# Four weight loads and eight context loads in another order on one DMA queue (a four-layer gated cross-attention kernel)

## The chip, the core and the metric

One Trainium2 chip, one of its cores. The time is device microseconds for one execution of the whole program. The kernel before took 2381.88 us, the median of three runs (2378.09 to 2385.84). One more execution was profiled and took 2372.64 us; every duration below is from that one.

## The reference

Sixteen sequences of 56 tokens with 256 channels pass four layers. Each layer adds a gated cross-attention to a context of 1500 positions with 64 channels for each sequence, and then a gated feed-forward part. Layers 0, 2 and 3 have a mixture of experts as feed-forward part, layer 1 an fp8-quantised matrix. What matters here is the seam inside layer 0 and what follows it:

```python
x = x + tanh(g_xattn[0]) * L0_xattn(layernorm(x), ctx_512, ...)
x = x + tanh(g_ffn[0])   * L0_ffn(layernorm(x), ...)
x = x + tanh(g_xattn[1]) * L1_xattn(layernorm(x), ctx_512, ...)

def L0_ffn(x):            # 16 experts, 4 for each token, and a shared expert for all tokens
    shared  = silu(x @ W1s.T) * (x @ W3s.T) @ W2s.T
    probs   = softmax(x @ Wg.T)
    combine = the four largest of probs, in place, 0 elsewhere
    h       = silu(x @ W1[e].T) * (x @ W3[e].T)          # every expert e
    return shared + sum over e of (h * combine[e]) @ W2[e].T
```

Layer 0's attention is causal and looks at the first 56 context positions only. Layers 1 to 3 look at all 1500, with a rotary embedding applied to the context first.

## The kernel before

The tokens lie as eight tiles of 112 (two sequences of 56 each), in SBUF all through the program (`x`). `kv` holds the whole context in SBUF, eight pairs of sequences, each 125 partitions by 1536 numbers (750 KB); each pair has one load.

**Layer 0's attention** (`attention_mha`) is a hand-written pipeline. Its loop `for i in range(NT + 1)` has nine turns; turn i makes scores of tile i and finishes tile i - 1, and moves the router of earlier tiles forward one phase at a time. Nearly every instruction is pinned with `in_order`, so an engine runs them in the order of the program text. Layer 0's attention needs only the small `k0` part of the context.

**The load queue.** Nearly all loads are issued by SyncE (SP), on one queue, in program order, while SP runs ahead of the compute: it waits only for room in the queue, for the completion of the load eight places before (there are eight completion semaphores for this queue, used in turn), and for buffers to come free. The order in layer 0 is: the tokens and small weights; sixteen clears of the DRAM table `rows` (`clear_rows`, L1177); in turn 2 the cosine and sine tables (`load_tables`, L889 and L890) and pairs 0 and 1; in turn 3 pairs 2 and 3; in turn 4 pairs 4 and 5 and then twelve head weights of layer 1 (`load_absorbed`, L233); in turn 5 pairs 6 and 7 (`load`, L893). Behind these `moe` issues the four loads of the shared expert, and then the experts' weights.

**Layer 0's experts** (`moe`). At its head the object `Shared` is made: it opens a pool "sw" on the right side of SBUF and issues four loads, gate/up weights `swgu` (L1413) and down weights `swd` (L1414) for two halves of the shared expert. The shared expert's work is cut into parts (`sh.parts`): `multiply` (L1429), `activate` (L1440, L1441) and `down` (L1446, L1448). The parts of the first four tiles are laid between the last phases of the router: `tail` holds the routers of tiles 4, 5 and 6, 7, which still have their transposes (L1062), logits (L1070), ranks, place counts (L1106, L1108) and scatters (L1121, on GpSimd) to do. The order at the seam is written out by hand:

```python
next(last); next(before); next(last); next(before)
now[0][0]()                      # shared expert, multiply: 8 matmuls on swgu, L1429
next(before)
for _ in range(4): next(last)    # last pair's transposes L1062, logits L1070, softmax
now[1][0]()
```

When the router has finished, `table` makes a list of expert tiles (up to 128 tokens of one expert). SP reads it (L1200) and loads for each tile the expert's weights `wgu` and `wd` (L1212, L1213), three tiles ahead, and the tile's rows `xrow` (L1219), which must wait for the scatters. TensorE turns the rows (L1226) and multiplies (L1238). Beside the tile loop DVE applies the rotary embedding to the context: `Roping.parts` (L901, L906, L909) takes the pairs in order 0 to 7. The head weights of layer 1 are used after the loop.

The pool "rope" is opened before everything of layer 0 and closed when layer 0 is done; it holds the two tables and a scratch tile.

Of the kernel before, what the change touches and what calls it, by code (L numbers as in the profile page):

```python
# [36 lines left out]
F32 = mybir.dt.float32  # L37
# [8 lines left out]
B, S, D = 16, 56, 256  # L46
# [19 lines left out]
def bcast(ap, axis, n):  # L66

    ap = ap.unsqueeze(axis)
    shape = list(ap.shape)
    shape[axis] = n  # L70
    return ap.to_broadcast(shape)
# [3 lines left out]
def flamingo_kernel(ctx: ExitStack, tc: tile.TileContext, d: dict, out: bass.AP):  # L75
    nc = tc.nc
# [9 lines left out]
    in_order = tc.keep_in_program_order  # L86
# [71 lines left out]
    class Normed:  # L158


        def __init__(self, pool):
            self.pool, self.kept = pool, {}
# [75 lines left out]
    def load_absorbed(l, g):  # L238
        loaded[l, g] = [
            load_heads(n, d[f"L{l}_{n}"], g)  # L240
            for n in ("wqr", "wkr", "wkc", "wq", "wkv", "wo")
        ]
# [136 lines left out]
                project_turned(*before)  # L379


    def attention_mha(router, roping):
        with ExitStack() as st:
            ap1 = st.enter_context(tc.tile_pool(name="a0c", bufs=1))
            ap = st.enter_context(tc.tile_pool(name="a0", bufs=2))
# [53 lines left out]
            for half in range(2):  # L439
# [4 lines left out]
                i = bcast(ps[0:DC, 0 : 4 * TP].rearrange("p (n s) -> p n s", s=S), 2, 2)  # L444
# [4 lines left out]
            def keys(t):  # L449
                ps = ps_k.tile([128, 512], F32, name="k_ps")[:, 0 : 4 * TP].rearrange("p (q n) -> p q n", q=4)  # L450
                for q in range(4):
                    in_order(nc.tensor.matmul(ps[:, q, :], wk[:, q, :], k0d[:, 2 * t : 2 * t + 2, 0, :], start=True, stop=True))
                made["k", t] = ps

            def keep_keys(t):
                ps = made.pop(("k", t))
                for h in range(4):
                    i = ps[32 * h : 32 * h + 32].rearrange("p q (b s) -> p q b s", b=2)
                    in_order(nc.scalar.copy(kbs[t % 2][32 * h : 32 * h + 32, :, :, h, :], i))

            def make_values(t):
                ps = ps_k.tile([TP, 512], F32, name="vb_ps")
                for b in range(2):
                    in_order(nc.tensor.matmul(
                        ps[:, b * D : (b + 1) * D], k0d[:, 2 * t + b].rearrange("p a s -> p (a s)"), wv, start=True, stop=True
                    ))
                made["v", t] = ps

            def keep_values(t):
                pv = made.pop(("v", t)).rearrange("p (b g a c) -> p b g a c", b=2, g=H // 2, a=2)  # L470
                for a in range(2):
                    in_order(nc.scalar.activation(vbs[t % 2][:, :, :, 16 * a : 16 * a + 16], pv[:, :, :, a, :], AF.Copy, scale=small[0:TP, C_M + a : C_M + a + 1]))
# [13 lines left out]
            def turn_normed(half):  # L486
                for k in range(2):
                    ps = (turns, misc)[k]()
                    for i in range(4):
                        in_order(nc.tensor.transpose(ps[:, i * TP : (i + 1) * TP], xn[:, i, k * 128 : (k + 1) * 128], ident[0:TP, 0:TP]))  # L490
                    copy = nc.vector.tensor_copy if k == 0 else nc.scalar.copy
                    in_order(copy(xnT[:, k, 4 * half : 4 * half + 4, :].rearrange("p t c -> p (t c)"), ps[:, 0 : 4 * TP]))

            def queries(half):
                for q in range(4):
                    ps = (turns, misc)[q % 2]()[:, 0 : 4 * TP]
                    for k in range(2):
                        in_order(nc.tensor.matmul(
                            ps,
                            wq[:, k, q * 128 : (q + 1) * 128],  # L500
                            xnT[:, k, 4 * half : 4 * half + 4, :].rearrange("p t c -> p (t c)"),
                            start=k == 0,
                            stop=k == 1,
                        ))

                    in_order(nc.scalar.mul(qT[:, q, half * 4 * TP : (half + 1) * 4 * TP], ps, 0.25))
# [84 lines left out]
            def route(i, *phases):  # L591

                for k in phases:
                    if (i - k) % 2 == 0 and 0 <= (i - k) // 2 < len(batches):
                        next(batches[(i - k) // 2])
# [3 lines left out]
            def at(i):  # L599
                return pairs[i] if 0 <= i < NT else None  # L600
# [10 lines left out]
            for i in range(NT + 1):  # L611
                new, cur = at(i), at(i - 1)
                if cur:
                    cur.turned()
                route(i, 2, 3, 5)
                if cur:
                    cur.keep_turned()
                if i + 1 < NT:
                    keep_keys(i + 1)
                if new:  # L620
                    keep_values(i)
                route(i, 4)
                if new:
                    new.scores()
                route(i, 3, 4)
                if new:
                    new.shift()
                    new.exps()
                if cur:
                    cur.values()  # L630
                route(i, 5)
                if cur:
                    cur.normalize()
                if i + 2 < NT:
                    keys(i + 2)
                if cur:
                    cur.turn_context()
                if i + 1 < NT:
                    make_values(i + 1)
                route(i, 5, 3, 4, 4)  # L640
                if cur:
                    cur.project()
                    cur.add()
                route(i, 3)
                if i == 0:
                    turn_normed(1)
                    queries(1)
                for _ in range(5):
                    next(clear, None)
                if i == 2:  # L650
                    roping.load_tables(nc.sync)
                if 2 <= i < 6:
                    roping.load(2 * i - 4, nc.sync)
                    roping.load(2 * i - 3, nc.sync)
                if i == 4:
                    load_absorbed(1, 0)
                    load_absorbed(1, 1)
# [224 lines left out]
    class Roping:  # L882
# [9 lines left out]
        def load(self, t, queue):  # L892
            in_order(queue.dma_start(kv[:, t], d["ctx"][t]))  # L893
# [283 lines left out]
            in_order(nc.sync.dma_start(rows[e * CT : (e + 1) * CT].rearrange("c p x -> p c x"), bcast(zero, 1, CT)))  # L1177
            yield

    def moe(r, nxt=None, tail=None, rest=None):  # L1180

        l = r.l
        n_e, ft, nf, top, n_t, n_sure = MOE[l]
# [2 lines left out]
        with ExitStack() as st:  # L1186

            right = st.enter_context(ExitStack())
            side = {"side": "right"} if l == 0 else {}
# [5 lines left out]
            pw, pp = pool("w", 4, **side), pool("", 3, **side)  # L1195
            ps_h = pool("h", 2 if l == 2 else 4, space=PSUM)
            ps_o = pool("o", 2, space=PSUM)
# [74 lines left out]
            if l == 0:  # L1272


                sh = Shared(pool, ps_h, ps_o, side)
                now = [part for e in range(2) for part in sh.parts(e, 0)]
                between = [part for e in range(2) for part in sh.parts(e, 1)]
                before, last = tail
                next(last)
                next(before)  # L1280
                next(last)
                next(before)
                now[0][0]()
                next(before)
                for _ in range(4):
                    next(last)
                now[1][0]()
                for _ in range(3):
                    next(last)
                next(last)  # L1290
                next(last)
                r.table()
            else:
                r.table()
# [42 lines left out]
            if l == 0:  # L1337
# [8 lines left out]
                rest = rest()  # L1346
# [55 lines left out]
    class Shared:  # L1402


        def __init__(self, pool, ps_h, ps_o, side):
            self.ps_h, self.ps_o = ps_h, ps_o
            self.pp = pool("s", 2, **side)
            pw = pool("sw", 1, **side)
            self.w = []
            for e in range(2):  # L1410
                wgu = pw.tile([128, 2, 2, 176], F32, name=f"swgu{e}")
                wd = pw.tile([88, 2, D], F32, name=f"swd{e}")
                in_order(nc.sync.dma_start(wgu, d["L0_wgu"][16 + e]))  # L1413
                in_order(nc.sync.dma_start(wd, d["L0_wd"][16 + e]))  # L1414
                self.w.append((wgu, wd))

        def parts(self, e, half):

# [138 lines left out]
    @contextmanager  # L1557
    def routed(l):
        with tc.tile_pool(name=f"r{l}c", bufs=1) as keep, ExitStack() as temporary:
            yield Router(l, keep, temporary)  # L1560

    with tc.tile_pool(name="rope", bufs=1) as rope, routed(0) as r:
        roping = Roping(rope)
        tail = attention_mha(r, roping)
        nxt = Next(1)
        moe(r, nxt, tail, roping.parts)
    with ExitStack() as keep:
        f1w = keep.enter_context(tc.tile_pool(name="f1w", bufs=1, reuse_waits="tile"))
        matrix = f1w.tile([128, 2, D], F32, name="w8"), f1w.tile([128, 4], F32, name="sc")
# [3 lines left out]
        nxt = Next(2)  # L1573
# [7 lines left out]
    with routed(2) as r:  # L1581
        attention_mla(2, nxt, r)
        nxt.whole.close()
        nxt = Next(3)
# [152 lines left out]
```

## Time and profile before

| | |
|---|---|
| median of three runs | 2381.88 us |
| the profiled execution | 2372.64 us |
| its span | 2370.8 us |
| mean granted TensorE clock | 0.971 |
| PE busy | 2226.7 us (94%) |
| DVE busy | 1556.8 us (66%) |
| ACT busy | 1232.3 us (52%) |
| POOL busy | 342.8 us (14%) |
| SP queue (q1), share of 16 DMA engines | 21.6% |
| bytes moved by DMA | 172.97 MB, mean 73 GB/s |

PE is TensorE, PEld its weight load (which overlaps PE), DVE VectorE, ACT ScalarE, POOL GpSimd, SPq the issuing of DMAs by SyncE. L12 is line 12 of the kernel. A row of a timeline gives the start in us, the duration in us, the engine, the line, the operation, what it writes and reads, how many instructions are merged, and in brackets how long the engine had been idle before and what ended that. A row of waits gives the waiting line, what it waited for, the sum in us, how often, and the longest. "PEclk" is the clock granted to TensorE as a share of full speed. The last figure of a DMA issue row is not shown for SP, so landing times are read from who waits for them.

### The profile page before, as it was taken

How to read it: one execution, taken by the hardware profiler on the slowest of the kernel's cores; microseconds unless marked ns; L12 is line 12 of the kernel's file. 1: busy time of each engine (PE TensorE's matmuls, PEld its weight loads, DVE VectorE, ACT ScalarE, POOL GpSimd, SP SyncE). 2: the span in 40 equal slices, each digit the busy share in tenths (PEclk: the TensorE clock that was granted, in tenths of full speed). 3: DMA queues.
4: the chain of work that ended last, by engine and by line, in shares of the span. 5: the costliest groups of instructions: out<-in, count | busy, mean ns of one | idle time of the engine just before them, and what ended most of it. 6: DMA issues, size and time to landing. Idle time of an engine off the chain costs nothing. (4 is left out here: it accounts for less than half of the span.)

```text
span 2370.8 us, 47911 instructions
## 1 busy us (share of the span) xinstructions
PE 2226.7 (94%) x17853; PEld 1603.2 (68%) x17858; DVE 1556.8 (66%) x3594; ACT 1232.3 (52%) x2703; POOL 342.8 (14%) x676
## 2 busy tenths in 40 slices
PE   8859998999999999999999999979899999999797
PEld 5626655777777775447777777745577777777454
DVE  5727545777777777667777777724577777777222
ACT  4403336666666663356666666513566666665131
POOL 1223600000000003420000000001001111111223
PEclk9769999999999999989999999999999999999799
DMA  9546761000000002200000000055101000000597
GB/s 244 184 138 193 207 166 64 9 22 21 22 21 22 21 23 69 66 17 22 23 24 13 21 22 23 11 202 159 34 21 30 29 20 26 25 28 16 158 289 209
DMA packets 114891, 172.97 MB, mean 73 GB/s; under 512 B 19258, under 2 KB 77635, under 8 KB 113628
## 3 DMA queue, kind: packets, MB, share of 16 engines
q1 hardware_dynamic: 105510, 151.35, 21.6%
q0 software_dynamic: 7600, 17.14, 2.2%
q8 instruction: 144, 2.36, 0.4%
q10 hardware_dynamic: 1542, 1.34, 0.2%
q14 instruction: 95, 0.78, 0.1%
HBM read 131.24 MB, written 40.48 MB: 72 GB/s over the span
## 5 line engine op out<-in xcount | busy, mean ns | idle before, releaser
L745 ACT ACTIVATE p<-s_ps,nm 128x500 f32<-128x500 f32 x504 | 335.7, 675 | 361.9 <-DVE nm L736 361.9
L722 PE MATMUL s_ps<-kvT,qT 64*128 64x500 f32 x2016 | 484.2, 607 | 11.4 <-ACT p L754 4.8
L796 PEld LDWEIGHTS m_ps<-pT,kv 125*64 125x64 f32 x8064 | 436.7, 137 | 65.8 <-issue 57.4
L734 DVE TENSOR_REDUCE part<-s_ps 128x1 f32<-128x500 f32 x504 | 340.3, 678 | 213.4 <-PE s_ps L722 213.0
L796 PE MATMUL m_ps<-pT,kv 125*64 125x128 f32 x8064 | 477.3, 275 | 1.8 <-ACT pT L789 1.2
L722 PEld LDWEIGHTS s_ps<-kvT,qT 64*128 64x128 f32 x2016 | 186.8, 189 | 196.1 <-issue 121.6
L784 PE MATMUL m_ps<-ident,p 128*125 128x128 f32 x2016 | 297.4, 282 | 0.2
L739 DVE TENSOR_REDUCE nm<-s_ps 128x1 f32<-128x1500 f32 x168 | 287.2, 1710 | 1.2 <-PE s_ps L722 1.2
L784 PEld LDWEIGHTS m_ps<-ident,p 128*125 128x125 f32 x2016 | 247.5, 187 | 35.5 <-issue 26.0
L754 ACT ACTIVATE p<-s_ps,nm 128x1500 f32<-128x1500 f32 x168 | 254.9, 1517 | 0.5 <-DVE nm L739 0.4
L784 PE MATMUL s_ps<-ident,p 128*125 128x128 f32 x2016 | 248.8, 273 | 0.3 <-ACT p L745 0.3
L784 PEld LDWEIGHTS s_ps<-ident,p 128*125 128x125 f32 x2016 | 233.7, 188 | 1.2 <-ACT p L745 0.5
L789 ACT COPY pT<-s_ps 125x512 f32<-125x512 f32 x336 | 181.0, 596 | 98.3 <-PE s_ps L784 82.3
L765 POOL TENSOR_TENSOR den<-den 128x1 f32<-128x1 f32 x168 | 32.7, 194 | 1210.2 <-ACT p L745 1209.9
L789 ACT COPY pT<-m_ps 125x512 f32<-125x512 f32 x336 | 185.2, 617 | 0.0
L807 DVE TENSOR_TENSOR ctxT<-m_ps,rep 64x128 f32<-64x128 f32 (+1 forms) x384 | 104.2, 271 | 88.1 <-PE m_ps L796 81.1
L1238 PE MATMUL gu_ps<-wgu,xT 128*128 128x448 f32 (+2 forms) x344 | 141.2, 537 | 20.1 <-DMA wgu<-in_L_wgu 13.7
L1243 DVE TENSOR_TENSOR act<-gu_ps,act 128x224 f32<-128x224 f32 (+2 forms) x78 | 31.2, 400 | 152.4 <-ACT act L1242 152.3
L787 DVE COPY pT<-m_ps 125x512 f32<-125x512 f32 x168 | 116.2, 692 | 10.1 <-PE s_ps L784 0.9
L314 ACT COPY qT<-q_ps 64x224 f32<-64x224 f32 x128 | 71.8, 561 | 97.1 <-PE q_ps L358 60.3
L1263 POOL DMA_INDIRECT results<-y,to x78 | 90.6, 1162 | 203.5 <-ACT y L1262 193.8
L787 DVE COPY pT<-s_ps 125x512 f32<-125x512 f32 x168 | 114.3, 681 | 0.0
(294 smaller groups left out, 2514.7 us busy)
## 6 DMA issues: line engine op xcount, KB each, us to landing
wgu<-in_L_wgu SPq DMA_DIRECT2D x36, 448.0 KB
rows<-zero SPq DMA_DIRECT2D x16, 899.5 KB
kvT<-turned_kv SPq DMA_DIRECT2D x16, 750.0 KB
wgu<-in_L_wgu SPq DMA_DIRECT2D x34, 352.0 KB
rep<-through SPq DMA_DIRECT2D x336, 32.0 KB
xrow<-rows SPq DMA_DIRECT2D x78, 128.5 KB
wgu<-in_L_wgu SPq DMA_DIRECT2D x8, 1024.0 KB
wd<-in_L_wd SPq DMA_DIRECT2D x36, 224.0 KB
```

The lines of the kernel that those rows point to most:

```text
L722: in_order(nc.tensor.matmul(o[:, 0 : 4 * KP], qT[64 * b : 64 * b + 64, t, j * QT : (j + 1) * QT], kvTs[t][64 * b : 64 * b + 64, z * 4 * KP ...
L734: in_order(nc.vector.tensor_reduce(self.part[:, z : z + 1], sp0[z][:, 0 : 4 * KP], AX.X, ALU.max))
L739: in_order(nc.vector.tensor_reduce(self.nm[1], sp1[:, :, 0 : 4 * KP], AX.XY, ALU.max, negate=True))
L745: in_order(nc.scalar.activation(self.p[0][:, 4 * z * KP : 4 * (z + 1) * KP], sp0[z][:, 0 : 4 * KP], AF.Exp, bias=self.nm[0], accum_out=sel ...
L754: in_order(nc.scalar.activation(self.p[1].rearrange("p (z c) -> p z c", z=3), sp1[:, :, 0 : 4 * KP], AF.Exp, bias=self.nm[1], accum_out=se ...
L784: in_order(nc.tensor.transpose(ps[:, c, :], self.p[b][:, k : k + KP], ident))
L787: in_order(nc.vector.tensor_copy(o, ps))
L789: in_order(nc.scalar.copy(o, ps))
L796: in_order(nc.tensor.matmul(self.pv[64 * b : 64 * b + 64, :], kv[:, self.t, c, b, :], self.pT[:, c, b, :], start=c == 0, stop=c == KC - 1))
L807: in_order(nc.vector.tensor_tensor(ctxs[self.t][64 * a : 64 * a + 64, b, lo - 448 * a : hi - 448 * a], self.pv[64 * b : 64 * b + 64, cols] ...
L1238: in_order(nc.tensor.matmul(ps[:, s, 0:n], xT[:, k, :], wgu[:, k, s * n : (s + 1) * n], start=k == 0, stop=k == 1))
L1263: i = nc.gpsimd.indirect_dma_start(flat, bass.IndirectOffsetOnAxis(ap=to[:, 0:1], axis=0), y, None, bounds_check=B * S * top - 1, oob_is_e ...
```

## The change

`Shared` is split in two. Its weight tiles are now made in the pool "rope" when the program begins (`__init__`), its four loads are issued by a method `load`, and what is left (`begin`) opens the pool for the intermediate tiles where the object was made before. The attention of layer 0 calls `sh.load()` in turn 2, ahead of the two tables. The context's pairs have new turns: pair 0 in turn 3, pair 1 in turn 4 (ahead of the head weights), pairs 2 and 3 in turns 5 and 6, pairs 4 and 6 in turn 7, pairs 5 and 7 in turn 8. The right-side pool "sw" is gone, and "rope" is 9,728 bytes per partition larger (two tiles of 2,816 bytes and two of 2,048). The instructions of PE, DVE, ACT and POOL and their order stay as they are; only SP's order differs.

```diff
-    def attention_mha(router, roping):
+    def attention_mha(router, roping, sh):
...
                 if i == 2:
+                    sh.load()
                     roping.load_tables(nc.sync)
-                if 2 <= i < 6:
-                    roping.load(2 * i - 4, nc.sync)
-                    roping.load(2 * i - 3, nc.sync)
+                if i > 2:
+                    roping.load(i - 3, nc.sync)
+                    if i > 6:
+                        roping.load(i - 1, nc.sync)
                 if i == 4:
                     load_absorbed(1, 0)
                     load_absorbed(1, 1)
...
-                sh = Shared(pool, ps_h, ps_o, side)
+                sh.begin(pool, ps_h, ps_o, side)
...
     class Shared:
-        def __init__(self, pool, ps_h, ps_o, side):
+        def __init__(self, keep):
+            self.w = [
+                (keep.tile([128, 2, 2, 176], F32, name=f"swgu{e}"), keep.tile([88, 2, D], F32, name=f"swd{e}")) for e in range(2)
+            ]
+
+        def load(self):
+            for e, (wgu, wd) in enumerate(self.w):
+                in_order(nc.sync.dma_start(wgu, d["L0_wgu"][16 + e]))
+                in_order(nc.sync.dma_start(wd, d["L0_wd"][16 + e]))
+
+        def begin(self, pool, ps_h, ps_o, side):
             self.ps_h, self.ps_o = ps_h, ps_o
             self.pp = pool("s", 2, **side)
-            pw = pool("sw", 1, **side)
-            self.w = []
-            for e in range(2):
-                wgu = pw.tile([128, 2, 2, 176], F32, name=f"swgu{e}")
-                wd = pw.tile([88, 2, D], F32, name=f"swd{e}")
-                in_order(nc.sync.dma_start(wgu, d["L0_wgu"][16 + e]))
-                in_order(nc.sync.dma_start(wd, d["L0_wd"][16 + e]))
-                self.w.append((wgu, wd))
...
-        roping = Roping(rope)
-        tail = attention_mha(r, roping)
+        roping, sh = Roping(rope), Shared(rope)
+        tail = attention_mha(r, roping, sh)
...
-        moe(r, nxt, tail, roping.parts)
+        moe(r, nxt, tail, roping.parts, sh)
```

More of the change, by code (lines that the diff above doesn't have):

```diff
@@ L1178, in clear_rows, with moe @@
             yield
-    def moe(r, nxt=None, tail=None, rest=None):
+    def moe(r, nxt=None, tail=None, rest=None, sh=None):
         l = r.l
```

## The prediction

> **What bounds the kernel now.** I read the page's slices first, then the waits of layer 0, then that stretch in windows and as a timeline, and last the load queue (SP) by itself.
>
> ```profile
> PE   8859998999999999999999999979899999999797
> DMA  9546761000000002200000000055101000000597
> ```
>
> One digit is 59.3 us (2370.8 / 40). PE is near full nearly everywhere, so TensorE bounds the kernel over most of the span; the lowest digit is slice 2, 118.5 to 177.8 us, the joint between layer 0's attention and its experts. The waits of the first 182 us name its hole:
>
> ```profile
> PEld sgu_ps L1429 <- DMA swgu<-in_L_wgu: 24.3, 1, 24.3
> PE sgu_ps L1429 <- DMA swgu<-in_L_wgu: 24.2, 1, 24.2
> ```
>
> One wait of 24.2 us, for the shared expert's gate/up weights. The windows (us, then busy time of PE, PEld, DVE, ACT, POOL, then the TensorE clock, DMA share, GB/s) show how empty it is:
>
> ```profile
> 110.00:115.00 5.00, 2.71 (x6) 1.36 (x6) 4.76 (x12) 1.90 (x3) 2.20 (x4) 0.50 0.60 203
> 120.00:125.00 5.00, 0.00 (x0) 0.00 (x0) 0.41 (x2) 0.00 (x0) 3.76 (x5) 0.50 1.00 254
> 135.00:140.00 5.00, 0.00 (x0) 0.00 (x0) 0.00 (x0) 0.00 (x0) 0.00 (x0) 0.50 0.31 129
> ```
>
> Only POOL does anything, and that ends by 129 us. Nothing runs beside this wait that could keep the time up. The timeline gives its edges:
>
> ```profile
> 116.30 0.53 PE L1108 MATMUL m_ps<-total,ones 112*112 112x16 f32 x2
> ...
> 119.67 0.73 DVE L1054 TENSOR_SCALAR xr<-x,mv,y 112x256 f32<-112x256 f32 x2
> ...
> 128.38 0.33 POOL L1064 COPY xr<-small 112x4 f32<-112x4 f32 x2
> 141.04 5.80 PE L1429 MATMUL sgu_ps<-xnT,swgu 128*88 128x448 f32 x8 [24.21 <-DMA swgu<-in_L_wgu]
> ...
> 156.79 0.93 POOL L1121 DMA_INDIRECT rows<-xr,sloti  x1 [28.08 <-issue]
> ...
> 179.09 0.38 PE L1226 MATMUL m_ps<-ident,xrow 128*128 128x128 f32 x2
> ```
>
> PE stops at 116.83 and resumes at 141.04. Behind the stopped matmul stand, on PE in order, the transposes of the last routed tokens (L1062), so the router's end, the table, and every expert tile are late with it. Why the weights are late is in the queue's own timeline:
>
> ```profile
> 66.01 17.70 SPq L893 DMA_DIRECT2D kv<-in_ctx  x6
> 83.76 14.27 SPq L233 DMA_DIRECT2D wqr<-in_L_wqr  x1
> ...
> 119.42 0.33 SPq L233 DMA_DIRECT2D wkr<-in_L_wkr  x1
> ...
> 121.75 0.81 SPq L893 DMA_DIRECT2D kv<-in_ctx  x2
> 122.68 0.35 SPq L1413 DMA_DIRECT2D swgu<-in_L_wgu  x1
> ...
> 170.51 2.97 SPq L1219 DMA_DIRECT2D xrow<-rows  x4
> ```
>
> They are issued at 122.68, last of all, behind two tables, eight context pairs of 750 KB and twelve head weights. wqr's 14.27 us of issuing is the queue being full. In the instruction listing each load also waits for the completion of the one eight places before it; SP's waits show 9.8 us of that (two waits on pairs), the last let go at 119.42.
>
> **The change, part by part.**
>
> *The four shared loads to the front.* They now stand directly behind the 16 row clears, at the place where the cosine table was issued at 62.62 us. The clears' rate lasts until about 71 us (244 GB/s, then 140 from 72). 2 x (352 + 176) KB = 1.08 MB at 244 GB/s take 4.4 us: landed by about 76, some 40 us before PE asks at 116.8. The whole 24.2 us wait goes. Nothing before 116 us waits for a table, a pair or a head weight, so what they are pushed back by costs nothing there.
>
> *What is late next.* (1) The shared matmul's other input, the first half of xnT, was made before the copy at 104.3 us that served the third pair of tiles, and the last a0 PSUM reader ends at 106.7; so it starts at 116.85. Its 8 matmuls take 5.80 us: until 122.65. (2) The transposes behind it need xr, ready at 120.40 and not moved: 2.2 us of margin. (3) POOL's scatters of the last pair (first at 156.79, so 132.6 after) need POOL, free at 128.71: margin 3.9 us. (4) The tile table comes from DVE, 159.5 before, 135.3 after; from there chain and queue order are as before. So everything from 141.04 on moves by 24.2 us, if the loads keep up.
>
> *The context behind them.* Queue order becomes: shared, tables, pairs 0 and 1, twelve head weights, pairs 2, 3, 4, 6, 5, 7. SP runs ahead of the compute, so "a turn each" changes order only, no start time. All the bytes are the same, so the backlog ends about when it did: traffic ran until about 142.5. What changes is who is last: a context pair, whose first reader (roping on DVE, 182.16 before, 158 after) takes the pairs one by one from number 0. But the expert weights (issued at 160.57 before, 136.4 after) and rows (170.51; 146.3 after) stand behind the pairs.
>
> [...] The row: at 135 to 140, when only pairs remain, the DMA share is 0.31 at 129 GB/s, that is five of 16 engines. [...] From landing times (pairs 4 and 5 let waits go at 112.91 and 119.42) it is 6.5 us with scatters beside it. I take 6.5. After: 71 + 4.4 (shared) + 6 (tables) + 2 x 6.5 + 4 (head weights) = 98, + 6 x 6.5 = 137; by equal bytes 142. SP is done issuing well before: the queue held about three pairs when wqr got in, so near 137 - 3 x 6.5 = 118, against 135.3.
>
> First expert weights then land 2 to 4 us after the last pair, about 141 to 146, needed at 179.94 - 24.2 = 155.7. First rows: before, issued 170.51, read by DVE at 172.84, needed by PE at 178.9; so after, needed by 154.7. Three tiles' weights (1.62 MB, a sixteenth per engine at 129/5 = 26 GB/s) add 3.9 us and the row load 2.3: the last pair must be down by 148.5. Margin 6 to 11 us. In the tile loop itself PE waits for wgu 6.8 us in six waits (180 to 320), but its loads are let go by the four weight buffers, so that loop moves as a whole. Cost taken: 0; bounds 0 and, if both estimates are 10 us low, 4.
>
> *Clock.* Row: 0.50 at 110 to 115, with PE half busy, so PE was already cold before the stop. [...] I take the row. Other end: the warm stretches of 148 to 156 and 170 to 180 come cold, about +10 us.
>
> *The pool.* 9,728 bytes per partition move from the right side into the rope pool, which ends with layer 0; left pools shift. Instruction order on PE, DVE, ACT and POOL is unchanged; a few releases differ (one later kvT load also waits for POOL; ACT's first kvT copies lose a wait). SP's waits at that load were 1.0 us in all, for a load fetched ahead: 0, bounds -1 and +1.
>
> Sum: -24.2. The profiled execution took 2372.64 us (span 2370.8): it would take 2348.4. The median of the runs shown is 2381.88, 9.2 higher; the hole does not depend on that, so 2381.88 - 24.2 = **2357.7 us**.
>
> **Rivals.** *Context tail takes part:* pairs need about 10 us each, the last lands near 160, rows come 12 us late: 2370. For it: five engines, last scatters beside them. Against: 6.5 us measured under scatters. *Another releaser:* the wait is put to the load that came last, but POOL ended at 128.7; if the matmul or what follows needs it, 141.0 - 128.7 = 12.3 gained: 2369.6. Against: the matmul reads only xnT and the weights. *Cold clock:* 24.2 - 10 = 14: 2368. *Slower:* the same tail, whole: one place, the expert loads behind pairs on five engines. It eats everything when the last pair lands 24.2 us past 148.5, at 172.7, (172.7 - 98) / 6 = 12.4 us a pair; at 13.5 us, 7 more: 2388. That is twice the row.
>
> **How the numbers follow.** Forecast 0.76, its own range 2347 to 2367 (runs shown spread 8 us); context tail 0.08; other releaser 0.06; cold clock 0.04; tail that cancels the gain 0.03; slower 0.03. A measurement tells about 0.3%, 7 us, from no change. Faster 0.94, same 0.03, slower 0.03. The three partial cases lie at 2368 to 2370, so the range is 2345 to 2372.
>
> **What would show it.** Right: no wait of L1429 on swgu, its first matmul at about 117, the last routing transposes near 122.5, first expert matmul near 156, shared loads down by 80; traffic near 130 GB/s until about 140. Wrong: PE waiting at L1226 or L1238 for xrow or wgu, SP still issuing pairs past 136, or a new hole between 117 and 156.

## The result, and the profile after

The change is faster, but by about half of what was forecast: 2369.18 us (median of 4 runs, 2367.27 to 2373.49) against 2383.86 us for the kernel before on the same chip (4 runs, 2378.09 to 2387.71). The ratio on record is 0.9949, 95% interval 0.9929 to 0.997, which is 12.2 us (7 to 17). It is an estimate over all the runs and not the quotient of the two medians, which lie 14.7 us apart. The forecast was 24.2. The profiled execution took 2373.49 us (span 2371.7, clock 0.972).

The page's slices of the changed kernel (59.3 us each, counted from 0) already say that the hole is not filled as it should be. Slice 2 of PE was 5 before:

```profile
PE   8878998999999999999999999979899999999697
DMA  9647561000000002200000000064001010000596
```

It rose to 7 only, and slice 3 fell from 9 to 8. The waits of the first 182 us of the changed kernel (engine, line, what it waited for, sum in us, times, longest) name no wait for `swgu` any more. They name others in its place:

```profile
PE m_ps L575 <- DVE sum_p L1079: 6.6, 3, 5.0
...
DVE den L569 <- remote: 5.5, 1, 5.5
...
DVE mx L537 <- remote: 5.1, 2, 3.6
...
PE m_ps L1142 <- DVE weight L1172: 3.8, 1, 3.8
...
DVE sloti L1119 <- DMA rows<-xr,sloti: 2.0, 1, 2.0
```

"remote" is a semaphore whose updater the profile does not show; `den` and `mx` are VectorE instructions that wait for TensorE's values (L561) and scores (L523). TensorE's own timeline at these two places:

```profile
89.85 0.72 PE L561 MATMUL m_ps<-vb,pT 112*64 112x34 f32 x19
91.03 0.19 PE L561 MATMUL m_ps<-vb,pT 112*64 112x34 f32 x1 [0.45 <-issue]
91.73 0.29 PE L561 MATMUL m_ps<-vb,pT 112*64 112x34 f32 x3 [0.51 <-issue]
93.17 0.26 PE L561 MATMUL m_ps<-vb,pT 112*64 112x34 f32 x2 [1.14 <-issue]
94.57 0.66 PE L561 MATMUL m_ps<-vb,pT 112*64 112x34 f32 x7 [1.14 <-issue]
...
115.23 1.93 PE L561 MATMUL m_ps<-vb,pT 112*64 112x34 f32 x32
122.14 0.66 PE L575 MATMUL m_ps<-ident,ctx 128*128 128x128 f32 x2 [4.98 <-DVE sum_p L1079]
...
128.65 6.10 PE L1434 MATMUL sgu_ps<-xnT,swgu 128*88 128x448 f32 x8
```

In other turns the 32 values matmuls take 1.08 to 1.93 us in one group. Here they come in five, with 3.2 us of gaps that nothing in the profile explains ("issue"). Behind the last group of L561 TensorE stands 4.98 us, where it stands 0.91 in the traces of both kernels on chip 8 below. It waits there for VectorE, whose `den` waits 5.5 us until 121.27, although the matmuls that it needs seem done at 117.16; why is not in the profile. I call these the two **holds**. The trace of the kernel before that the prediction was made from has neither. The sixth turn (from its L549 to the next) lasted 10.2 us there and 15.8 here, and from the last turn's L549 to the first shared matmul being ready it was 12.8 there and 16.6 here. That is 9.4 us; another 2.8 were there before the sixth turn (TensorE's clock was 0.50 from 60 to 65 us here and 1.00 before). Together with 0.4 us regained between, the shared expert began at 128.65 us and not at 116.85: it waited for nothing, and still came 11.8 us late. So the change saved 141.04 - 128.65 = 12.4 us there, between these two profiled executions. The weights were not what it was late for.

### The profile page after: what moved, and what is told of

It reads as the page before. It is cut to its first block, busy times and chain, and to the rows that moved or that the text cites. A ratio compares the mean times of both kernels' runs of the same rounds, so it can differ in the third digit from the quotient of the medians.

```text
span 2371.7 us, 47925 instructions
## 1 busy us (share of the span) xinstructions
PE 2234.8 (94%) x17858; PEld 1609.6 (68%) x17858; DVE 1557.6 (66%) x3594; ACT 1231.0 (52%) x2703; POOL 341.0 (14%) x676
## 5 line engine op out<-in xcount | busy, mean ns | idle before, releaser
L724 PE MATMUL s_ps<-kvT,qT 64*128 64x500 f32 x2016 | 482.5, 605 | 11.8 <-ACT p L756 5.1
L809 DVE TENSOR_TENSOR ctxT<-m_ps,rep 64x128 f32<-64x128 f32 (+1 forms) x384 | 104.4, 272 | 90.0 <-PE m_ps L798 79.5
```

What stands on the lines that cost most here:

```text
L724: in_order(nc.tensor.matmul(o[:, 0 : 4 * KP], qT[64 * b : 64 * b + 64, t, j * QT : (j + 1) * QT], kvTs[t][64 * b : 64 * b + 64, z * 4 * KP ...
L809: in_order(nc.vector.tensor_tensor(ctxs[self.t][64 * a : 64 * a + 64, b, lo - 448 * a : hi - 448 * a], self.pv[64 * b : 64 * b + 64, cols] ...
```

## Experiments

Three explanations stood at first. **A:** the holds belong to the new load order. **B:** they fall on executions of any kernel, so the kernel before has them too and hides them in its wait for the weights. **C:** what is missing is lost behind the seam, where scatters and expert weights share the DMA engines with the late context pairs.

### The same two kernels again, and two halves of the change (one chip, number 6)

Both kernels unchanged:

> The kernel before once more, for a second trace of it. Its first profiled execution (2372.6 us) lay some 11 us below the median of its runs, so 2378 to 2388 us here, with the 24 us wait on the shared weights (about 117 to 141) again. Theory A (TensorE holds come with the new load order): no hold of 3 us or more before 117 us. Theory B (such holds fall on some executions of any kernel): one or two holds of 3 to 5 us somewhere.

> The changed kernel once more, unchanged. In its first trace TensorE's results came late twice in attention (90.4 to 94.6 and 117.2 to 121.3), and the first shared matmul started at 128.65 where 116.85 was forecast. Theory A (the holds belong to the new load order): both holds again at the same places, start near 128, ratio 0.993 to 0.997. Theory B (chance of that execution): no holds or at other places, start between 117 and 120 in this trace, ratio still about 0.995 if every execution has some. Theory C (the loss lies behind the seam, in scatters and expert loads on five DMA engines): start near 117, but first expert tile later than 158.

The shared loads alone, with the pairs in their old turns:

```diff
                 if i == 2:
                     sh.load()
                     roping.load_tables(nc.sync)
-                if i > 2:
-                    roping.load(i - 3, nc.sync)
-                    if i > 6:
-                        roping.load(i - 1, nc.sync)
+                if 2 <= i < 6:
+                    roping.load(2 * i - 4, nc.sync)
+                    roping.load(2 * i - 3, nc.sync)
```

> Shared loads ahead of the tables as in the change, but the context's pairs in their old turns: six pairs, then the head weights, then pairs 6 and 7. Theory A (head weights arriving beside attention at 84 to 98 us cause the holds): no holds before 117, full gain of 24 us, ratio about 0.990. Theory B: as the change, ratio 0.995. Theory C: as the change or worse, since the last pairs still stand before the expert loads: ratio 0.995, expert loads behind two pairs.

The change, with each pair's load cut into one of 112 partitions and one of 13:

```diff
-            in_order(queue.dma_start(kv[:, t], d["ctx"][t]))
+            for lo, hi in ((0, 112), (112, KP)):
+                in_order(queue.dma_start(kv[lo:hi, t], d["ctx"][t, lo:hi]))
```

> [...] The backlog should end by about 115 to 120 us, not 142. Theory C: the lost part comes back, ratio about 0.990. Theory A: holds change with the traffic around them; ratio between 0.990 and 0.997. Theory B: ratio 0.995.

Measured against 2372.57 us of the kernel before (20 runs): the change 2363.81, ratio 0.9964 (0.9946 to 0.9982); the shared loads alone 2360.93, 0.9947 (0.9928 to 0.9966); the split 2362.6, 0.9955 (0.9938 to 0.9973). The intervals overlap, so nothing is shown to be gained by the new order of the pairs or by the cut once the shared loads are ahead: these carry the gain. The new order of the pairs alone was not run. All four traces have both holds, the kernel before too; A falls. TensorE's timeline of that trace of the kernel before:

```profile
111.21 1.93 PE L561 MATMUL m_ps<-vb,pT 112*64 112x34 f32 x32
118.16 0.66 PE L575 MATMUL m_ps<-ident,ctx 128*128 128x128 f32 x2 [5.02 <-DVE sum_p L1077]
...
124.30 0.54 PE L1108 MATMUL m_ps<-total,ones 112*112 112x16 f32 x2
132.79 5.62 PE L1429 MATMUL sgu_ps<-xnT,swgu 128*88 128x448 f32 x8 [7.96 <-DMA swgu<-in_L_wgu]
```

The same wait for the same weights is 7.96 us here and was 24.2 in the first trace, of the same kernel. Both its ends moved: TensorE was ready 8.0 us later (124.84 for 116.83), and the weights landed 8.2 us earlier (132.79 for 141.04); of this 6.8 were there when SP got to the tables, at 55.84 us and not at 62.62. The 8.0 us that TensorE lost do not show in the kernel's time (2367.44 here, 2372.64 in the first trace), because the wait takes up what is lost ahead of it. The change takes the wait away and lays the holds bare. On this chip its first shared matmul came at 124.7, 8.1 us earlier, and the first expert weights were issued 8.2 us earlier (144.3 for 152.4): all of the wait, and nothing lost by C.

### Split loads, a shifted TensorE stream, memsets among the scatters (chip 11)

The same cut of the pairs' loads in the kernel before, with nothing else changed, and with the shared loads ahead and the pairs in their old turns:

> The kernel before, with one edit: each context pair's load is cut in two, 112 partitions and 13, so that most of its bytes can use all sixteen DMA engines. The four shared loads stay last in the queue. Theory 1 (in most executions the hole of the shared weights is 8.0 us, 124.84 to 132.8, and it is made by loads that run on five engines ahead of them): the split loads finish earlier, the shared weights land before 124.8, the wait of the first shared matmul goes, and the time falls like that of the change, about 8 us (ratio about 0.9965). Theory 2 (the queue ahead of the shared loads is bound by bytes or by its completion semaphores): the shared weights still land near 132, the wait stays near 8 us, ratio 0.999 to 1.001.

> The shared loads ahead, the pairs in their old turns, and each pair cut into 112 and 13 partitions: the two parts of the earlier runs that looked best, together. If the loss of the change lies behind the seam (weights and rows of the first expert tiles behind loads on five engines), this is the best of all: 3 to 5 us under the shared loads alone, near 2356. If all of the gain there is is the 8.0 us of the hole, it is the same as the shared loads alone: near 2361, ratio 0.994 to 0.996.

Two probes of the holds, on the kernel before. The first puts 64 tiny matmuls at the start of TensorE's stream, the second 30 memsets on GpSimd behind the first scatter:

```diff
+            idle = ap1.tile([128, 16], BF16, name="idle")
+            in_order(nc.vector.memset(idle, 0.0))
+            ps = turns()
+            for _ in range(64):
+                in_order(nc.tensor.matmul(ps[0:16, 0:16], idle, idle, start=True, stop=True))
             for half in range(2):
                 ps = turns()
```

> The kernel before, with 64 tiny matmuls of 16 columns put into TensorE's stream at the start of layer 0's attention, while TensorE waits for the first loads. They move everything behind them 128 instructions (a weight load and a matmul each) further down TensorE's program. Four traces show TensorE held up twice, inside the values matmuls of the sixth turn (L561, from about 86.7 to 90) and after those of the last turn (112.8 to 117.3). If TensorE's instruction supply makes the holds, they move to other instructions, about 128 earlier in the program (into the fifth and the seventh or eighth turn). If they belong to the work or to what runs beside it, they stay at the values matmuls of the sixth and the last turn.

```diff
                     self.sent.append(i)
                     in_order(i)
+                    if self.l == 0 and t == 0 and u == 0 and j == 0:
+                        idle = pool.tile([128, 256], F32, name="idle")
+                        for _ in range(30):
+                            in_order(nc.gpsimd.memset(idle, 0.0))
```

> The kernel before, with 30 memsets of 0.33 us put on GpSimd between the first scatter of the first routed pair (78.0 us) and its seven others, so that these run about 10 us later, from about 88 to 98. If the scatters beside it hold TensorE up in the sixth turn (86.7 to 90), this hold goes or moves to what TensorE does from 88 to 98. If TensorE is held at that place of its own program, whatever GpSimd does, the hold stays at the values matmuls of the sixth turn.

Against 2370.17 us before (11 runs), the split alone took 2347.3, ratio 0.9906 (0.9887 to 0.9925): 22.3 us, nearly three times what theory 1 expected. Shared loads and split together took 2352.07, 0.9915 (0.9898 to 0.9933), no better. The probes took 2371.71 and 2372.04. None of the four traces has a hold. So the probes told nothing of their cause, but the miss on the split told where to look: either the holds go with the program, or with the chip.

The second probe does not do what was meant, either. GpSimd's timeline shows the memsets laid between the scatters, and only the eighth scatter late (the last row is TensorE's wait for the weights):

```profile
78.72 1.00 POOL L1121 DMA_INDIRECT rows<-xr,sloti  x1 [68.19 <-DVE v L140]
79.73 0.34 POOL L1131 MEMSET idle<- 128x256 f32 x1
80.24 0.95 POOL L1121 DMA_INDIRECT rows<-xr,sloti  x1 [0.17 <-issue]
...
87.43 0.94 POOL L1121 DMA_INDIRECT rows<-xr,sloti  x1 [0.17 <-issue]
...
98.20 0.95 POOL L1121 DMA_INDIRECT rows<-xr,sloti  x1 [0.16 <-issue]
...
132.82 4.84 PE L1433 MATMUL sgu_ps<-xnT,swgu 128*88 128x448 f32 x8 [11.97 <-DMA swgu<-in_L_wgu]
```

So it would not have tested the scatters on a chip with holds. But its edit delays TensorE ahead of the wait: the turn before the last took 17.2 us here and 11.5 in the first probe, and TensorE was ready at 120.8 us and not at 116.4. The wait was 12.0 us and not 19.2 (the weights landed 2.8 us earlier, too), and the time was the same (2372.04 and 2371.71 us, one run each): the wait took the delay in.

The windows of the split kernel (busy time of PE, PEld, DVE, ACT, POOL, then clock, DMA share, GB/s) show what the cut does:

```profile
100.00:105.00 5.00, 4.41 (x54) 3.64 (x52) 3.27 (x12) 1.35 (x3) 3.78 (x5) 0.77 1.00 240
105.00:110.00 5.00, 1.52 (x6) 0.82 (x6) 4.76 (x12) 1.90 (x3) 4.04 (x6) 0.91 0.99 303
110.00:115.00 5.00, 4.17 (x12) 2.67 (x13) 3.67 (x21) 0.00 (x0) 0.00 (x0) 0.50 0.31 105
```

The queue runs at a share of 0.99 to 1.00 and 240 to 303 GB/s where the pairs ran at 0.31, five of 16 engines by that share, and 129 (first profile, 135 to 140 us). The large loads are down by about 112 us, and the shared expert begins at 112.3 without a wait, although its weights still stand last in the queue. So the run shows that the weights were late because of how the pairs' loads were shaped: it removes the same wait by another way. It fits the five engines that the prediction read from the row; why a pair's load uses five is not shown. A cut into two loads that would both stay narrow was not run, so the width is not told apart from having two loads for each pair.

### Does a hold go with the program or with the chip? (chip 2)

> The kernel before, unchanged, profiled on the same chip as the next three. TensorE was held up twice (L561 of the sixth turn, and behind the last L561) in all five traces of one session, whatever was changed there, and in none of the four of the next session. Theory P (the holds go with the chip that the program runs on): the four kernels of this call either all show both holds or none of them does. Theory Q (the holds go with the program): this kernel and the change show them, the split loads don't. In either case the wait of L1429 ends when the shared weights land, near 133 (131 to 142), and the time is near 2370, because the hole takes the holds in.

> The changed kernel again, on the same chip as the others of this call. If the hole of the kernel before is what the change is worth, its gain is the wait that the kernel before shows in this call: about 8 us (ratio 0.996 to 0.997) with the holds, 13 to 19 us (ratio 0.992 to 0.9945) without them, since then TensorE is ready for the shared weights near 116.8 to 120 and no longer near 124.8. If the gain stays near 9 to 12 us without the holds, something behind the seam takes the rest.

> The kernel before with each pair's load cut into 112 and 13 partitions, again. In the session before it was 22.9 us faster than before, and TensorE, never held, began the shared expert at 112.3 us without a wait. With the holds it should begin near 124 and gain about 8 to 12 us (ratio 0.995 to 0.997); without them about 22 (ratio 0.990 to 0.992).

> The shared loads alone ahead, the pairs in their old turns, again. It was 12.5 us faster than before in the session with holds. Theory P: with holds about the same; without them 16 to 22 us faster, like the change but for the little that the order of the pairs costs.

All four have both holds, the split too, which had none on chip 11: Q falls and P stands. Against 2377.36 us (17 runs): the change 2366.88, ratio 0.9952 (0.9937 to 0.9968); the split 2363.07, 0.9939 (0.992 to 0.9958), where it had 0.9906 (0.9887 to 0.9925) without holds; the shared loads alone 2367.75, 0.9955 (0.9937 to 0.9973). The kernel before waited 15.28 us here: ready at 125.1, weights at 140.4. The first shared matmul of the change came 16.2 us earlier, but the first expert weights only 12.9 earlier. Of the 3.3 between, 2.7 are in one row of the changed kernel's timeline. First TensorE in the kernel before, then the changed kernel:

```profile
140.41 4.85 PE L1429 MATMUL sgu_ps<-xnT,swgu 128*88 128x448 f32 x8 [15.28 <-DMA swgu<-in_L_wgu]
```

```profile
124.20 5.52 PE L1434 MATMUL sgu_ps<-xnT,swgu 128*88 128x448 f32 x8
...
141.34 0.17 DVE L1119 CAST sloti<-slot 112x8 int32<-112x8 f32 x1 [2.71 <-DMA rows<-xr,sloti]
...
142.30 0.50 PE L1142 MATMUL m_ps<-ones,rep 112*112 112x1 f32 x2 [4.58 <-DVE weight L1172]
```

So on this chip C has a part: the last scatter places (`sloti`) have one buffer, and their cast waits until the scatters of the tiles before have landed.

### A chip without holds, with both kernels (chip 8)

> The kernel before, unchanged, profiled on the same chip as the next three. Either the two holds of TensorE are there (then the first shared matmul could start near 124 to 125), or they are not (then near 117 to 120, as in the trace that the prediction was made from). In both cases it starts when the weights land, at 132 to 141, so the time is 2367 to 2385 with or without them.

> The changed kernel on the same chip. If the chip shows no holds, this is the case that the prediction assumed, with both kernels alike: the first shared matmul starts near 117 to 120 and the gain is the wait of the kernel before in this call less 0 to 6 us for the context's tail, 10 to 20 us, ratio 0.9915 to 0.996. With holds it starts near 124 to 128, and the gain is 8 to 12 us again, ratio 0.995 to 0.997.

> The kernel before with 64 tiny matmuls at the start of TensorE's stream. On a chip with holds: if the instruction supply makes them, they move to instructions some 128 earlier in the program (before the values matmuls of the sixth and of the last turn); if they belong to the work or to what runs beside it, they stay at these matmuls. On a chip without holds it tells nothing of them, as in its first run.

> The kernel before with 30 memsets on GpSimd between the first scatter of the first routed pair and its seven others, which then run at about 88 to 98 us and no longer at 78 to 88. On a chip with holds: if the scatters make the first hold, it goes from the values matmuls of the sixth turn (86 to 90 us); if not, it stays there. On a chip without holds it tells nothing of them, as in its first run.

None of these four traces has a hold, and the case that the prediction assumed is there at last. TensorE and the first expert weights of SP in the kernel before, then in the changed one:

```profile
113.76 0.54 PE L1108 MATMUL m_ps<-total,ones 112*112 112x16 f32 x2
139.15 4.86 PE L1429 MATMUL sgu_ps<-xnT,swgu 128*88 128x448 f32 x8 [24.86 <-DMA swgu<-in_L_wgu]
...
157.74 0.38 SPq L1212 DMA_DIRECT2D wgu<-in_L_wgu  x1
...
175.78 0.38 PE L1226 MATMUL m_ps<-ident,xrow 128*128 128x128 f32 x2
```

```profile
115.22 5.43 PE L1434 MATMUL sgu_ps<-xnT,swgu 128*88 128x448 f32 x8
...
122.46 3.22 PE L1434 MATMUL sgu_ps<-xnT,swgu 128*88 128x448 f32 x8
...
133.77 0.51 PE L1142 MATMUL m_ps<-ones,rep 112*112 112x1 f32 x2 [5.14 <-DVE weight L1172]
...
137.62 0.38 SPq L1214 DMA_DIRECT2D wgu<-in_L_wgu  x1
...
156.10 0.39 PE L1228 MATMUL m_ps<-ident,xrow 128*128 128x128 f32 x2
```

The wait is 24.86 us, and the change takes all of it: 139.15 to 115.22 is 23.9. Of this, 3.8 are given back by the first expert weights (issued at 137.6 for 157.7), and the rest arrives: the first expert turn 19.7 us earlier, layer 1's first scores 20.0 earlier, the time 2353.03 against 2376.89 (11 runs), ratio 0.9917 (0.9891 to 0.9942), 19.7 us (the medians lie 23.9 apart). What is given back is again mostly one wait; GpSimd and VectorE in the changed kernel:

```profile
126.41 1.03 POOL L1123 DMA_INDIRECT rows<-xr,sloti  x1 [0.30 <-issue]
...
132.81 0.17 DVE L1119 CAST sloti<-slot 112x8 int32<-112x8 f32 x1 [3.31 <-DMA rows<-xr,sloti]
```

GpSimd was done with the scatter at 127.4, but its data had landed only at 132.8, 6.4 us behind its start. The context pairs that still move beside it seem to have a share in this. The issue rows of the eight scatters of the third pair of tiles (count, median us from issue to landing) read, in the changed kernel here (114 to 128 us) and in the shared loads with split pairs on chip 11 (117 to 131 us):

```profile
rows<-xr,sloti POOLq DMA_INDIRECT x8, 6.1
```

```profile
rows<-xr,sloti POOLq DMA_INDIRECT x8, 2.6
```

The load queue moved 1.55 MB in the first of these stretches and nothing in the second, and there the cast of the last places (132.01 us, last scatter started at 128.78) waits for nothing. The five traces of the change fall the same way. By the context pairs' packets in the load queue (6,144 bytes, 1,000 of them), the last pair was down at 145.2, 143.2 and 145.5 us in the three where this cast waits (it ran at 145.6, 141.3 and 132.8), and at 137.4 and 134.9 in the two where it does not (139.2 and 138.6). So C has a part, by way of the scatters. An experiment that changes the pairs' traffic alone, on one chip, was not run. The probes again ran without holds (2383.04 and 2365.1 us, one run each) and again told nothing of them. Here too the probe with the memsets delayed TensorE (ready at 125.4 us, 114.9 in the other) and was not the slower one.

### Four buffers for the scatter places (chip 0)

```diff
-            sloti = pool.tile([TP, 2, top], I32, name="sloti")[:, 0:n]
+            sloti = pool.tile([TP, 2, top], I32, name="sloti", bufs=4)[:, 0:n]
```

> The changed kernel once more, as the neighbour of the next run on one chip. Without holds: the last cast of the scatter places (L1119) waits 2 to 3.5 us for a scatter of the pair of tiles before, the first expert turn (L1228) stands about 41 us behind the first shared matmul, and the ratio to before is about 0.992. With holds: a wait of 0 to 2.7 us and ratio 0.995 to 0.997.

> The changed kernel with four buffers for the scatter places (sloti) in place of one, so that the last pair's cast L1119 need not wait until the scatters of the pair before have landed. If this wait is what the change loses behind the seam, the first expert turn comes as much earlier as the neighbour's wait is long (0 to 3.5 us), and the time falls by 2 to 4 us against the neighbour where that waits 2 us or more. If the loss is in the late context pairs themselves, the wait goes but the first expert turn does not move, since the weights or rows of the first tiles then end last: 0 us.

Inconclusive. Both traces have holds, and with the holds the change itself had no wait at L1119 (cast at 138.6 us), so there was nothing to take away: 2362.08 us against 2363.69, ratios to before 0.9961 (0.9946 to 0.9977) and 0.9971 (0.9957 to 0.9986), first expert turn at 162.0 and 161.7. Whether more buffers bring back the 3.3 us where the wait exists was not seen.

### The sessions side by side

| chip | holds | before: ready, weights land, wait | change: first shared matmul | expert weights issued earlier by | ratio of the change |
|---|---|---|---|---|---|
| not recorded | no before, yes after | 116.8, 141.0, 24.2 | 128.65 | 9.9 | 0.9949 (0.9929 to 0.997) |
| 6 | in 4 of 4 traces | 124.8, 132.8, 8.0 | 124.7 | 8.2 | 0.9964 (0.9946 to 0.9982) |
| 2 | 4 of 4 | 125.1, 140.4, 15.3 | 124.2 | 12.9 | 0.9952 (0.9937 to 0.9968) |
| 8 | 0 of 4 | 114.3, 139.2, 24.9 | 115.2 | 20.1 | 0.9917 (0.9891 to 0.9942) |
| 0 | 2 of 2 | not profiled | 124.0 | | 0.9971 (0.9957 to 0.9986) |
| 11 | 0 of 4 | | | | (split alone 0.9906) |

In microseconds (one minus the ratio, by the time before) the three full rows gain 8.5 (4 to 13), 11.4 (8 to 15) and 19.7 (14 to 26). The medians differ by 8.8, 10.5 and 23.9. The column before the ratio, 8.2, 12.9 and 20.1, is what is left of the wait (8.0, 15.3, 24.9) after what is given back up to that point. The gain goes with it, but the intervals of chips 6 and 2 overlap, and that the numbers agree to 1.5 us is more than such intervals can show.

## Why the prediction was wrong in the size

*Which wait bounds the seam, and that the shared loads at the front remove it:* right in every trace; no profiled execution of the change waits for `swgu`.

*The size of it, "So everything from 141.04 on moves by 24.2 us":* this is the term that failed. It came from "it starts at 116.85", the end of the chain in front of the wait, and from "the hole does not depend on that", which set the profiled execution's wait beside the median of the others. In the changed kernel's trace the first shared matmul came at 128.65 us, so 12.4 us moved and 11.8 did not; 9.4 of these are the two holds. The wait is a difference of two times, and neither was the same from trace to trace. Over the four traces of the unchanged kernel TensorE was ready at 114.3, 116.8, 124.8 and 125.1 us and the weights landed at 139.2, 141.0, 132.8 and 140.4, so the wait was 8.0 to 24.9. The time of these executions (2374.4, 2372.6, 2367.4 and 2383.0) does not go with when TensorE was ready, because the wait absorbs the holds; the shortest is that in which the weights landed first. The profile that I had was of the kind without holds, and the profiled execution of the changed kernel has them. On a chip where both kernels run without, the step comes true to 0.3 us (24.2 forecast; 24.9 waited, 23.9 moved, as the start came 0.9 later), and 20.1 of it are left when the first expert weights are issued.

*What is late next, margin (3):* wrong link. I took "POOL free at 128.71" as the end of the scatters, with 3.9 us of margin. What the last pair of tiles needs is not GpSimd but the landing of the earlier scatters, which frees the one `sloti` buffer; on chip 8 that came 6.4 us behind the last scatter's start. The old wait hid it. VectorE waited 2.0, 2.7 and 3.3 us for it in three traces of the change and not at all in two.

*The context behind them, "Cost taken: 0; bounds 0 and 4":* the measured giving back of 0 to 3.8 us by the time the first expert weights are issued lies inside the bounds, but mostly for the reason just told and not for late weights or rows. The last pair was down at 134.9 to 145.5 us, in three of five traces later than both estimates (137 and 142), and always ahead of the 148.5 that the prediction allowed. It took the pairs to be slowed by the scatters beside them (6.5 us for each, the distance between two landings in the first profile, 112.91 and 119.42); that scatters land later beside pairs was not in it. On chip 8 the first expert turn (156.10) followed directly on the shared expert's last matmuls, which ended at 156.26 by their rows (152.98 + 3.28; ends are modelled). The order of the pairs is not shown to cost anything in the kernel's time: the shared loads alone and the change overlap on both chips where both ran.

*Clock:* the row that I took was right, and no gain by the clock is seen. It was 0.50 ahead of the first shared matmul with the wait and without it (chip 8: 130 to 135 us in the kernel before, 110 to 115 in the changed one). The first 8 shared matmuls took 5.80 us in the profile that was shown, 4.86 behind the 24.9 us wait on chip 8 and 5.43 without any wait there: filling the hole saved no cold start. The other end, that later stretches come cold, did not happen either: the second group of 8 took 3.22 us as before, at a clock of 1.00 (chip 8, 120 to 125 us). The 10 us put on it were an estimate, and no run shows them.

*Rivals:* three of them stood at 2368 to 2370 us, and the 2369.18 that was measured lies there by chance, for a reason that none of them gives. The context tail has the right neighbourhood, but it needs a last pair near 160 us, and the latest was 145.5; another releaser of L1429 and a tail that cancels the gain are refuted by every trace.

*What stays open:* what makes the holds. The order of loads, the size of the loads and the kernel are excluded. TensorE's instruction supply and GpSimd's scatters, both beside the holds, were probed twice on chips without holds, and the probe of the scatters left seven of eight nearly where they were, so neither is excluded. Nor is the profile's own recording, for the reason in the last section. Nor is chip told from session, as each session ran on one chip. Why the weights land up to 8 us apart in executions of one kernel was not tried.

## What to carry to other kernels

A wait is the distance between two times, and its length in one profile is what removing it is worth only if both are stable: take a second profile before pricing it, because a wait that many runs share also hides whatever goes wrong in front of it. When a stall is removed, follow every buffer of the next stage to the landing of the DMA that frees it, not to the end of the engine that issued it. And where a queue is late because of a few loads that use a third of the engines (a share of 0.31 here), reshaping these loads can do as much as reordering the queue: cutting 125 partitions into 112 and 13, with nothing moved, removed the same wait on chip 11.

## What was not expected of the hardware

In layer 0's attention TensorE was held twice, for some 4 to 6 us each by the lengths of the turns, at the same two places of the program in all ten traces of chips 6, 2 and 0 and in the first trace of the change, and in none of the eight of chips 11 and 8. In the first hold its small matmuls come, behind a first longer group, in groups of one to thirteen with gaps of mostly 0.4 to 1.2 us; in the second, and in ten of the eleven traces in the first too, VectorE waits up to 5.7 us for a semaphore whose updater the profile does not show. The same eleven traces have one more such wait late in the program (VectorE's `ctxT`, L807 to L809, at 2100 to 2200 us, 3.4 to 4.3 us), in both kernels.

The two kinds of traces differ in one thing more. The nine without holds give the scatters of the whole program a median time from issue to landing (2.6 to 3.4 us); the eleven with holds give none, for the scatters or for anything else that GpSimd issues. So something differs beside TensorE, in the execution or in what was recorded of it. The ratios of the change fall the same way, 0.9949 to 0.9971 with holds and 0.9917 without, though only one chip stands for the latter. Every run of the experiments has a span and a clock on record, so nothing here shows whether an execution that is not recorded has the holds.
